# The first MLP unit of a convolution-attention kernel: the GELU of hidden block 0 moved behind the second group's outputs

## The chip, the cores and the metric

The kernel runs on one core of a Trainium2 chip. The metric is device time in microseconds (us) of one whole execution; the figure for a kernel is the median of its runs. All times inside an execution are counted from the start of the profiled span.

## The reference

The computation is two layers on an image batch `x` of 2 x 512 x 32 x 32 in float32. Layer 0 is an attention with deformed sampling points and a learned position bias, followed by an MLP over the channels. Layer 1 is a plain self-attention over the 1024 positions. The change lies in the MLP of layer 0:

```python
xn2 = _bn(x, bn2_g, bn2_b)
h1 = gelu(einsum('bchw,oc->bohw', xn2, mlp_w1) + mlp_b1, approximate=False)
return x + einsum('bchw,oc->bohw', h1, mlp_w2) + mlp_b2
```

`mlp_w1` is 2048 x 512 and `mlp_w2` is 512 x 2048, so the MLP takes 512 channels to 2048 hidden ones and back, for 2 images of 1024 positions.

## The kernel before

**Units.** The work goes attention of layer 0 (about 1900 us), its output projection, the MLP, then layer 1. The MLP is cut into eight units: image `b` (2) by hidden quarter `p` (4 quarters of 512 hidden channels). The loop at `for i, (b, p) in enumerate(units)` calls `layer1` for the 512 hidden channels and `layer2` for their share of the output. The change concerns unit 0 only, where `early` is true (`i == 0`).

**Products by quarters.** Every matrix product here is a 2 x 2 block product done with seven block products instead of eight, the operands being sums and differences of the quarters. Products are numbered 1 to 7, and `PARTS` says which two operands belong to each. A hidden quarter is kept in the tile `hm`, as `c11, c12, c21, c22` (256 channels by 512 positions each), with two more blocks, `r5` and `r3`, for partial results. `c11` is block 0, `c21` is block 2.

**Two levels in `layer1`.** Outer product 2 is done plainly: in unit 0 by `first`, which runs before everything else and copies its result into `r3` (L1133). The six other outer products go in three groups of two, (1,6), (4,7), (5,3), called groups 0, 1 and 2 below. For a group, `twice` runs seven inner products, called q1 to q7, on TensorE (L160), each 2 matmuls of 128x128 by 256 positions; a float32 matmul shows as two records in the profile, so a q is 4 records. The results lie in two PSUM tiles for each group, and the q's are added up in PSUM: q6 is added onto q1's result, q7 onto q6's, q4 onto q7's; q5 and q3 share the other tile with q2. So each result is read out before the next is added: q1 by ScalarE (L166), q2 by VectorE, q6 by ScalarE (L170), q7 by ScalarE (L172) and VectorE, q4 by ScalarE (L176), q3 by VectorE. For group 2 the target of these reads is `r5` and `r3`.

**What follows a group.** `done(0)` adds `c11` to `c12`. `done(1)` makes `c22`, then `c21`, and calls `gelu(2)`, `done(2)` makes the rest and calls `gelu(3)` and `gelu(1)`. A `gelu` is two ScalarE activations of 128x512 (L1092). In unit 0, `merge` adds `r3` (the result of outer product 2) to `c11` on VectorE, and calls `gelu(0)`.

**What sets the order.** Each step has a due time: the inner products have `7 * group + STEPS`, and further steps are put in by `fills`, a list of pairs of a due time and a function. All are sorted by due time and then written out:

```python
STEPS = ((0, 1), (1, 2), (3, 6), (4, 5), (6, 7), (9, 4), (12, 3))
todo = [(7 * g + t, g, q) for g in range(len(sets)) for t, q in STEPS]
todo += [(t, None, fill) for t, fill in fills]
for _, g, q in sorted(todo, key=lambda e: e[0]):
    with tc.issue_after(newest(mybir.EngineType.PE)):
```

So `merge` at 13.5 stands between q7 of group 1 (13) and q1 of group 2 (14); q4 of group 1 is at 16, q6 of group 2 at 17, q3 of group 1 with `done(1)` at 19, q7 of group 2 at 20. A scheduler then sets the final order on each engine; each engine works through its own in that order. PSUM tiles come in turn from four buffers, so a new tile waits for the last reader of the one four before. In unit 0 the scheduler also puts matmuls of `layer2` (L1073) between the last inner products of group 2.

In the program as built, ScalarE's order around the change is: q7 of group 1 (L172), q4 of group 1 (L176), the load of the activation table for GELU, `gelu(0)` (two instructions), q1 of group 2 (L166), q6 of group 2 (L170), q7 (L172), q4 (L176), `gelu(2)`, `gelu(3)`, `gelu(1)`.

**Weights.** For the next unit, SyncE's queue loads `mlp_w1` (L982) and copies parts of it into `w1e` (L992), and GpSimd's queue forms sums in place by DMAs that add (L975). The copies wait until the current unit's matmuls have read `w1e` for the last time.

Of the kernel before, what the change touches and what calls it, by code (L numbers as in the profile page):

```python
# [57 lines left out]
def conv_seq_kernel(ctx: ExitStack, tc: tile.TileContext, x, xt, kst, pst, cst, vec, wsm, outw, w1, w2, wl, wlt, brow, out):  # L58
# [15 lines left out]
    def col(name, i=0):  # L74
        return vs[:, VOFF[name] + i : VOFF[name] + i + 1]
# [45 lines left out]
    def spread(x, which=range(4)):  # L121
        for i in which:
            if i % 2 == 0:
                o, u = ((4, 0), (1, 3))[i // 2]
                nc.vector.tensor_tensor(x[o], x[u], x[1], ALU.subtract)  # L125
            else:
                o, u, v = ((5, 4, 3), (6, 5, 2))[i // 2]
                nc.vector.scalar_tensor_tensor(x[o], x[u], -1.0, x[v], ALU.mult, ALU.subtract)
# [7 lines left out]
    def plus(out, a, b_, op=ALU.add):  # L136
        nc.vector.tensor_tensor(out, a, b_, op)  # L137
# [46 lines left out]
    def inner_w(w, we, at=slice(1, 7), e=slice(0, 6)):  # L184
        return [w[:, at, k, P * n : P * n + P] for k, n in AT_W] + [we[:, e, j, :] for j in range(3)]

    def inner_x(x, xe, at=slice(1, 7), e=slice(0, 6)):
        return [x[:, at, k, 256 * n : 256 * n + 256] for k, n in AT_X] + [xe[:, e, j, :] for j in range(3)]
# [779 lines left out]
    with ExitStack() as top, tc.tile_pool(name="wp", bufs=1) as wp:  # L968
# [100 lines left out]
        def product(w, x):  # L1069
            def go(ps, a, b_):  # L1070
                for m in range(2):
                    for k in range(2):
                        nc.tensor.matmul(  # L1073
                            ps[:, m, :], w[:, a, k, m * P : (m + 1) * P], x[:, b_, k, :],
                            start=(k == 0), stop=(k == 1),
                        )
            return go
# [11 lines left out]
        def layer1(p, we, w, xb, xe, hm, others=(), early=False):  # L1089
            def gelu(blk, src, scale=1.0):  # L1090
                for m in range(2):
                    nc.scalar.activation(  # L1092
                        hm[:, blk, m, :], src[:, m, :], AF.Gelu,
                        bias=col("mb1", 4 * p + 2 * (blk // 2) + m), scale=scale,
                    )

            c11, c12, c21, c22, r5, r3 = (hm[:, j] for j in range(6))

            def weights(q, j):
                a = FIRST_W[PARTS[q][0]]  # L1100
                return [inner_w(w, we, a, a - 1)[j]]

            def moving(q, j):
                b_ = FIRST_X[PARTS[q][1]]
                return [inner_x(xb, xe, b_, b_ - 1)[j]]

            def dest(g, m, h):
                return hm[:, 2 * g : 2 * g + 2, m, 256 * h : 256 * h + 256]

            def done(g):  # L1110
                if g == 0:
                    plus(c12, c12, c11)
                elif g == 1:
                    plus(c22, c22, c12)
                    plus(c21, c21, c22)
                    gelu(2, c21, -1.0)
                else:
                    plus(c22, c22, r5)
                    gelu(3, c22, -1.0)
                    plus(c12, c12, r5)  # L1120
                    plus(c12, c12, r3)
                    gelu(1, c12)

            def second():
                ps = mq.tile([P, 2, 512], F32, tag="ps2", name="sw")
                product(w, xb)(ps, 0, 0)
                plus(c11, c11, ps)
                gelu(0, c11)

            def first():  # L1130
                ps = mq.tile([P, 2, 512], F32, tag="ps2", name="sw")
                product(w, xb)(ps, 0, 0)
                nc.scalar.copy(r3, ps)  # L1133

            def merge():
                plus(c11, c11, r3)
                gelu(0, c11)

            plain = ((-1, first), (13.5, merge)) if early else ((21, second),)
            twice(mq, ((1, 6), (4, 7), (5, 3)), weights, moving, dest, done, (*plain, *others))  # L1140
            spread([hm[:, j] for j in range(7)])

# [52 lines left out]
        for i, (b, p) in enumerate(units):  # L1195
# [9 lines left out]
            wa, we, wb = wts.pop((b, p))  # L1205
            hm = cp.tile([P, 7, 2, 512], F32, tag="big", name="hm")
            layer1(p, we, wa, xb, xe, hm, ((4, lambda: part(1)), (10, lambda: part(2))) if p == 0 else (), i == 0)
            if i == NU:
                with tc.issue_after(newest(mybir.EngineType.DVE)):
# [384 lines left out]
```

## Time and profile before

| | |
|---|---|
| median of 3 runs | 2625.18 us (2624.24 to 2625.37) |
| profiled execution, its own time | 2626.42 us |
| span in the profile (first to last instruction) | 2624.7 us |
| TensorE busy | 2597.7 us, 99% |
| VectorE busy | 2308.9 us, 88% |
| ScalarE busy | 1748.3 us, 67% |
| GpSimd busy | 977.8 us, 37% |
| mean granted TensorE clock | 0.998 |

Busy times are summed over the span; the granted clock is a share of full speed. TensorE's idle time is found in the view of the waits, its place in the timeline, and what it hung on in the chain of waits, which follows the last instruction back to what released it. In the timeline a row is: start, duration, engine, line, operation, output <- input, shape, count, and in brackets the idle time just before with what ended it. PEld is TensorE's loading of weights.

### The profile page before, as it was taken

What the parts mean: (1) busy time and instruction counts of PE and PEld (TensorE: products, weight loads), DVE (VectorE), ACT (ScalarE), POOL (GpSimd) and SP (SyncE); (2) the same over time, 40 slices, a digit from 0 to 9 for tenths busy, and PEclk for the clock granted to TensorE, in tenths of its full rate; (3) what the DMA queues carried; (4) which work ended last, traced back from release to release, by engine and by line L of the source; (5) the groups of instructions that cost most, each with busy time, mean ns of one, the idle gap of its engine ahead of it and who ended that gap; (6) DMA issues with size and microseconds to landing.
All of it is one profiled execution on the core that took longest, in us unless ns stands there. A gap on an engine that the chain in (4) does not pass through costs nothing.

```text
span 2624.7 us, 48900 instructions
## 1 busy us (share of the span) xinstructions
PE 2597.7 (99%) x19648; PEld 1005.3 (38%) x19648; DVE 2308.9 (88%) x1462; ACT 1748.3 (67%) x2325; POOL 977.8 (37%) x1121
## 2 busy tenths in 40 slices
PE   9999999999999999999999999999999999999999
PEld 3332322232333233322333332332355665646556
DVE  7999999999999999999999999898776587666656
ACT  5887898888887888888787777777633242224041
POOL 1344544444444444444444444333422333200100
PEclk9999999999999999999999999999999999999999
DMA  5898988999999999899898999787777768400202
GB/s 189 173 193 186 214 181 183 197 193 206 189 191 195 190 204 193 182 188 202 187 203 182 194 193 195 162 181 166 155 195 160 155 139 177 90 16 0 73 0 56
DMA packets 177522, 428.27 MB, mean 163 GB/s; under 512 B 29936, under 2 KB 78208, under 8 KB 174608
## 3 DMA queue, kind: packets, MB, share of 16 engines
q0 software_dynamic: 107392, 273.09, 58.1%
q1 hardware_dynamic: 69472, 151.75, 17.4%
q8 instruction: 155, 2.54, 0.4%
q14 instruction: 71, 0.58, 0.1%
q10 hardware_dynamic: 432, 0.31, 0.0%
HBM read 82.16 MB, written 6.55 MB: 34 GB/s over the span
## 4 chain that ended last, share of the span: by engine, by line
PE 75%; DVE 10%; issue 7%; DMA 4%; POOL 2%; ACT 2%; DVEq 0%; ACTq 0%; POOLq 0%; SPq 0%
PE ps L693 47%; PE sw L1073 7%; PE sw L160 7%; PE sw L1244 7%; DVE h L676 4%; PE sw L1020 2%; PE sw L1342 2%; DVE ub L713 2%; DMA u<-uc 1%; POOL u L732 1%; PE psg L595 1%; DMA u<-u 1%; PE sim L823 1%; DVE uo L713 1%; DVE hm L137 1%
## 5 line engine op out<-in xcount | busy, mean ns | idle before, releaser
L693 PE MATMUL ps<-h,cw 128*32 128x512 f32 x16384 | 1774.9, 593 | 10.8 <-ACT rx L703 7.9
L676 DVE CUSTOM_DVE_ANT_1 h<-ta,tb 128x4096 f32<-128x4096 f32 (+1 forms) x257 | 1131.0, 4402 | 20.3 <-PE ps L693 16.8
L693 PEld LDWEIGHTS ps<-h,cw 128*32 128x32 f32 x16384 | 525.9, 110 | 1228.8 <-issue 1134.5
L703 ACT ACTIVATE rx<-ps,sc 128x1024 f32<-128x1024 f32 x512 | 568.3, 1110 | 159.6 <-PE ps L693 100.1
L732 POOL DMA_DIRECT2D u<-u x397 | 409.1, 1511 | 15.0 <-DMA u<-ub 12.1
L705 ACT ACTIVATE ub<-ps,sc 128x1024 f32<-128x1024 f32 x256 | 308.2, 1204 | 83.8 <-PE ps L693 83.4
L713 DVE SCALAR_TENSOR_TENSOR ub<-rx,sc,ub 128x1024 f32<-128x1024 f32 x256 | 327.2, 1278 | 10.5 <-ACT ub L705 10.5
L715 POOL DMA_DIRECT2D uo<-ub x127 | 112.5, 886 | 582.8 <-DVE ub L713 536.0
L1073 PE MATMUL sw<-hm,w2t 128*128 128x512 f32 x448 | 194.3, 593 | 0.2 <-DVE hm L125 0.2
L705 ACT ACTIVATE uo<-ps,sc 128x1024 f32<-128x1024 f32 x128 | 154.1, 1204 | 42.1 <-PE ps L693 41.0
L713 DVE SCALAR_TENSOR_TENSOR uo<-rx,sc,uo 128x1024 f32<-128x1024 f32 x128 | 163.6, 1278 | 5.0 <-ACT uo L705 5.0
L732 POOL DMA_DIRECT2D u<-uc x126 | 126.3, 1246 | 23.5 <-DMA u<-uc 22.0
L715 POOL DMA_DIRECT2D uc<-ub x64 | 56.9, 889 | 196.9 <-DVE ub L713 156.0
L137 DVE TENSOR_TENSOR hm<-hm,sw 128x512 f32<-128x512 f32 x79 | 57.6, 732 | 79.0 <-PE sw L160 54.4
L1073 PEld LDWEIGHTS sw<-hm,w2t 128*128 128x128 f32 x448 | 84.9, 190 | 103.9 <-issue 97.3
L715 POOL DMA_DIRECT2D u<-ub x64 | 56.6, 884 | 167.5 <-DVE ub L713 163.9
L732 POOL DMA_DIRECT2D uc<-uo x63 | 100.3, 1593 | 21.1 <-DMA uc<-uo 20.8
L732 POOL DMA_DIRECT2D uc<-uc x63 | 106.3, 1688 | 2.3 <-DMA uc<-ub 2.3
L1408 POOL DMA_DIRECT2D xs<-rs x6 | 7.2, 1200 | 258.8 <-DVE rs L137 258.8
L656 ACT ACTIVATE ta<-fb,vs 128x512 f32<-128x512 f32 (+1 forms) x65 | 89.7, 1382 | 6.8 <-DMA fb<-fdr 6.8
L732 POOL DMA_DIRECT2D u<-uo x63 | 85.4, 1355 | 20.6 <-DMA u<-uo 16.2
L705 ACT ACTIVATE uc<-ps,sc 128x1024 f32<-128x1024 f32 x64 | 77.0, 1203 | 22.4 <-PE ps L693 14.1
(295 smaller groups left out, 2621.9 us busy)
## 6 DMA issues: line engine op xcount, KB each, us to landing
uo<-ub POOLq DMA_DIRECT2D x127, 512.0 KB, 5.4
fb<-fdr SPq DMA_DIRECT2D x64, 512.0 KB, 6.2
u<-ub POOLq DMA_DIRECT2D x64, 512.0 KB, 6.5
uc<-ub POOLq DMA_DIRECT2D x64, 512.0 KB, 6.1
u<-u POOLq DMA_DIRECT2D x63, 256.0 KB, 7.0
u<-uo SPq DMA_DIRECT2D x63, 256.0 KB, 5.7
u<-uo POOLq DMA_DIRECT2D x63, 256.0 KB, 7.1
uc<-uc POOLq DMA_DIRECT2D x63, 256.0 KB, 7.9
```

The source lines that it names most:

```text
L137: nc.vector.tensor_tensor(out, a, b_, op)
L160: nc.tensor.matmul(bank[:, e, :], w, x, start=(q in (1, 2, 5) and e == k == 0), stop=True, skip_group_check=True,)
L656: nc.scalar.activation(ta.rearrange("p j x -> p x j")[:, :, j0:j1], fb[:, 0, :, j0:j1], AF.Identity, bias=col("cb1"), scale=col("w1x"),)
L676: nc.vector._custom_dve(TENSOR_ADD_SAT, out=h1[:, y : y + step].rearrange("p y t x -> p (y t x)"), in0=a.unsqueeze(1).to_broadcast([P, ste ...
L693: nc.tensor.matmul(ps[32 * q : 32 * q + 32, h, :], cw2[:, 32 * z : 32 * z + 32], h1[:, 16 * h : 16 * h + 16, q, :], start=True, stop=True,)
L703: nc.scalar.activation(o, ps, AF.Relu, bias=sc[:, 4 + z : 5 + z])
L705: nc.scalar.activation(o, ps, AF.Relu, bias=sc[:, 4 + z : 5 + z], scale=sc[:, z : z + 1])
L713: nc.vector.scalar_tensor_tensor(r[1], r[0], sc[:, z : z + 1], r[1], ALU.mult, ALU.add)
L715: nc.gpsimd.dma_start(out=sums[s][1], in_=sums[s][3], accum_op=ALU.add)
L732: nc.gpsimd.dma_start(out=out, in_=in_, accum_op=ALU.add)
L1073: nc.tensor.matmul(ps[:, m, :], w[:, a, k, m * P : (m + 1) * P], x[:, b_, k, :], start=(k == 0), stop=(k == 1),)
L1244: nc.tensor.matmul(ps[:, m, :], w[:, a, k, c + m * P : c + (m + 1) * P], x[b_][:, k, :], start=(k == 0), stop=(k == nk - 1),)
```

## The change

In unit 0, `merge` is split: the addition of `r3` to `c11` keeps its due time of 13.5, and `gelu(0)` gets a due time of its own, 19.5, behind `done(1)` at 19 and ahead of q7 of group 2 at 20. Nothing is added or removed in the computation, and the other seven units are untouched.

```diff
-            def merge():
-                plus(c11, c11, r3)
-                gelu(0, c11)
-
-            plain = ((-1, first), (13.5, merge)) if early else ((21, second),)
+            plain = ((21, second),)
+            if early:
+                plain = (-1, first), (13.5, lambda: plus(c11, c11, r3)), (19.5, lambda: gelu(0, c11))
             twice(mq, ((1, 6), (4, 7), (5, 3)), weights, moving, dest, done, (*plain, *others))
             spread([hm[:, j] for j in range(7)])
```

In the program as built, the order changes on ScalarE alone, and there in one place: after q4 of group 1 come now q1 of group 2 (L166), the table load, the first half of `gelu(0)`, q6 of group 2 (L170), the second half of `gelu(0)`, and then q7 (L172) as before. `gelu(2)` still follows q4 of group 2. The instructions on TensorE, VectorE, GpSimd and SyncE keep their order. L166 now waits itself for the addition on VectorE, since it overwrites `r3`.

## Prediction

> **What bounds the kernel now.** I read the page's busy shares first, then TensorE's waits, then the chain of waits and the timeline around the change, and last the granted clock in a few stretches.
>
> ```profile
> span 2624.7 us, 48900 instructions
> PE 2597.7 (99%) x19648; PEld 1005.3 (38%) x19648; DVE 2308.9 (88%) x1462; ACT 1748.3 (67%) x2325; POOL 977.8 (37%) x1121
> ```
>
> TensorE is busy 99% of the span: only what takes idle time from it, or lets it run faster, shortens the kernel. Its waits (total us, times, longest):
>
> ```profile
> PE ps L693 <- ACT rx L703: 7.9, 14, 1.9
> PE sw L160 <- ACT hm L166: 3.8, 1, 3.8
> ```
>
> The longest single wait of the whole execution is 3.8 us, once, and it lies at the change. The chain of waits from 1955 to 1990 us shows what it hung on:
>
> ```profile
> 1954.98 7.35 PE sw L160 x34
> 1962.34 0.02 issue
> 1962.36 0.60 ACT hm L176
> 1962.96 0.02 issue
> 1962.97 1.28 ACT L1092
> 1964.26 0.01 issue
> 1964.27 1.33 ACT hm L1092 x2
> 1965.60 0.48 ACT hm L166
> 1966.08 0.04 issue
> 1966.12 6.39 PE sw L160 x16
> 1972.52 1.00 PE sw L1073 x2
> ```
>
> TensorE stops at 1962.32. ScalarE then does four things in a row: q4 of group 1 (L176), the table load, both halves of gelu(0), and q1 of group 2 (L166), on which q6 of group 2 is to be added. The reader is to see that TensorE waits only for the last of these. Also that 16 records then take 6.39 us, 0.40 each, where the 34 before take 7.35, 0.216 each. The stretches (length, busy time of each engine, granted clock, DMA) tell why:
>
> ```profile
> 1811.14:1814.55 3.41, 1.52 (x16) 0.29 (x12) 2.53 (x3) 1.98 (x2) 2.50 (x3) 1.00 1.08 201
> 1961.33:1964.74 3.41, 0.99 (x5) 0.54 (x3) 1.33 (x2) 2.35 (x3) 0.85 (x1) 1.00 0.41 71
> 1964.74:1968.15 3.41, 2.02 (x5) 1.67 (x6) 0.69 (x1) 1.33 (x3) 0.00 (x0) 0.50 0.31 52
> 1968.15:1971.57 3.42, 3.42 (x10) 2.70 (x9) 0.00 (x0) 0.59 (x1) 0.00 (x0) 0.50 0.00 0
> ```
>
> From 1964.74 to 1971.57 the clock is 0.50. The wait costs twice: once as idle time, once as a slow restart. The wait of 1.89 us in the first row (TensorE busy 1.52 of 3.41) left the clock at 1.00.
>
> **What the Trainium skill says.** "TensorE: Matmul & The Clock Gate", Part 1, says that TensorE's clock halves after a free-running window of about 3.4 us with little activity and returns after one busy window. The trace agrees: the slow stretch is 6.83 us, two windows, after a window busy for 0.99 us; a window busy for 2.02 us did not end it. "ScalarE: Activation LUTs", What ACT_TABLE_LOAD costs, gives 1283 ns for a table load, as here (1.28 us), and a drain of 1380 ns, of which nothing shows: GELU starts 0.01 us behind the load. "Perfetto Trace Analysis", Tensor Engine Instruction, says that ScalarE and VectorE work strictly in order, and TensorE pulls only weight loads ahead. So L166 could not pass gelu(0); the trace shows it standing there.
>
> **The change, part by part.** It adds and removes no instruction. Of the three moved (the table load and gelu(0)'s two activations), none issues a DMA; the built order of TensorE, VectorE, GpSimd and SyncE is unchanged.
>
> *L166 ahead of the load and gelu(0).* L176 ends at 1962.96. L166 must now wait itself for the addition of r3, which runs on VectorE from 1961.44 for 1.22, to 1962.66: it is done. L166 takes 0.59 (0.562 to 0.592 in the three seen nearby), 1962.97 to 1963.56; with the 0.04 seen before, TensorE resumes at 1963.60 instead of 1966.12: **2.52 us** less idle time. The wait falls to about 1.28 us, inside the 1.89 that kept the clock.
>
> *The slow restart.* At full clock the 16 records to the end of q7 of group 2 take 16 x 0.216 = 3.46, to 1967.06. The next matmul (L1073, layer2's product 1) takes the buffer that VectorE frees by reading q3 of group 1. Before, the timeline has it begin at 1972.39 (the chain's 1972.52 is the modelled end of the record ahead), 0.99 after q3's last record gave way to the next at 1971.40. Now q3 is through after 12 records, at 1963.60 + 2.59 = 1966.19; plus 0.99 is 1967.18. So this matmul moves from 1972.39 to 1967.18, by 5.21 us: the 2.52 above and **2.69 us** from the clock.
>
> *What is now late behind gelu(0)'s first half.* The load runs 1963.56 to 1964.84, the first half (0.71) to 1965.56. q6's evacuation L170 is queued behind it; it was ready about 1.1 us after q6 began (1.17 and 1.06 in groups 0 and 1), at 1964.7. It runs 1965.56 to 1966.15, and q7 of group 2, which waits for it, is due on TensorE at 1966.19: cost nothing, by 0.04 us. If that cover fails, the wait is at most the 0.85 us by which L170 starts late. The second half ends at 1966.87; its readers are layer2's product 1 with its second half, after 1967.18 + 0.86 + 0.86, and L172, ready at 1966.19 + 1.16 = 1967.35. Both are covered, by 2.0 and 0.5 us. VectorE's read of q2, which q5 waits for, runs 1963.59 to 1964.28, q5 is due at 1964.46.
>
> *Whether the gain lasts.* gelu(2) began 3.96 us after q3 of group 1 (1971.40 to 1975.36), nearly all VectorE work; it would end at 1966.19 + 3.96 + 1.33 = 1971.5, and its product was reached at about 1977.8, now 1972.6. The copies of unit 1's `w1e` start behind the last read of `w1e` (1975.94 before, SyncE at 1976.13), so they move along. The in-place sums of `w1t` have fixed times, the last issued at 1962.91, and land some 3.3 us later, at 1966.2; the copies now come at 1970.9. To the end of the MLP and beyond TensorE's waits behind 1980 sum to 1.6 us, all on VectorE, which moves along. So I give nothing back.
>
> The sum is -5.21 us against the profiled execution (2626.42 us in all, 2624.7 of it span, 1.72 around it). The median of the timed runs is 1.24 lower; the same difference gives 2625.18 - 5.21 = **2620.0 us**. The bound of 0.2%, about what a measurement of this kernel can tell from no change, is 5.25 us here: the forecast lies on it.
>
> **The unknown: the clock's window.** An execution may have its windows elsewhere. A boundary 0.39 to 1.7 us ahead of the restart gives two slow windows, and a loss of half of 6.83 less that, 2.6 to 3.2 us (the profile's was 1.38 ahead, 2.7); one slow window costs 3.41 / 2 = 1.7; with the wait shared evenly between two windows there may be no drop, 0. I take the profile's, and keep 0 and 3.2 as ends; a loss below nothing is excluded, as the new wait is shorter.
>
> **The rivals.** (1) *One slow window* in most timed runs: gain 2.5 + 1.7 = 4.2, 2621.0 us. For it: the median lies 1.24 below the profiled execution; against it: profiling itself may cost that. (2) *Only the idle time goes* (no drop in the timed runs, or the clock still falls at 1.28 us): 2622.7. Against it: the row at 1811. (3) *Slower: gelu(0) really runs behind gelu(2)*, as the due times are written. Then product 1, due at 1967.18, waits for gelu(2) to end at 1971.5 and gelu(0)'s 1.33, to 1972.9; q4 and q3 of group 2 stand behind it. That is 5.7 us of wait and, being above 3.8, a new slow restart of 2.7: 8.4 lost for 5.2 gained, 2628.4. It decides once gelu(0) is later than 1972.4. Against it: the built order has gelu(0) around L170, ahead of L172. (4) *Nothing moves*, because the freed time is lost to a later wait, such as w1e's landing: 2625.2. Against it: that chain follows TensorE.
>
> **How the numbers follow.** Two slow windows saved, 5.1 to 5.7: 0.57, of which 0.45 above the bound. One window: 0.28. Idle time only: 0.08. Slower: 0.04. Nothing: 0.03. So faster 0.45, same 0.51, slower 0.04. The range goes from 5.7 and some noise of the runs (0.5) to just short of the case of idle time only: 2618.9 to 2622.4.
>
> **What would show it.** In the profile after, TensorE's wait on L166 should be about 1.3 us; L166 should start at about 1962.97, the table load behind it; no stretch around 1966 with clock 0.50; L1073's first matmul at about 1967.2; the span near 2619.5. A new wait of TensorE on L170, or a longer one on gelu, would make it wrong, as would a half clock that stays.

## The result, and the profile after

| | before | after |
|---|---|---|
| median of 22 runs each, us | 2625.17 (2623.59 to 2626.99) | 2620.51 (2619.63 to 2622.44) |
| span of the profiled execution, us | 2624.7 | 2618.7 |

The ratio of after to before is 0.9983, with a 95% interval of 0.9976 to 0.9989: 4.66 us less, 0.18%. The interval, 2.9 to 6.3 us, excludes no change; it does not tell whether the gain is above or below 0.2%.

The page of after opens with the same shares, and with one instruction more than before. That one is a semaphore instruction of ScalarE at L166, which now waits itself for the addition on VectorE:

```profile
span 2618.7 us, 48901 instructions
PE 2596.1 (99%) x19648; PEld 1003.4 (38%) x19648; DVE 2310.0 (88%) x1462; ACT 1746.8 (67%) x2325; POOL 981.0 (37%) x1121
```

TensorE's waits (total us, times, longest). The wait on L166 is down from 3.8 to 1.2 us, and none on L170 has come in its place:

```profile
PE ps L693 <- ACT rx L703: 7.9, 14, 1.9
...
PE sw L160 <- ACT hm L166: 1.2, 1, 1.2
```

The chain of waits around the change (start, length, what):

```profile
1954.81 7.57 PE sw L160 x35
1962.38 0.02 issue
1962.40 0.35 ACT hm L176
1962.75 0.15 issue
1962.89 0.59 ACT hm L166
1963.48 0.04 issue
1963.53 3.72 PE sw L160 x16
1967.25 1.04 PE sw L1073 x2
```

The table load and gelu(0) have left the chain; only L176 and L166 stand in it. The 16 records take 3.72 us instead of 6.39. The clock stays at 1.00 (stretches: length, busy time of PE, PEld, DVE, ACT, POOL, granted clock, DMA):

```profile
1960.38:1963.79 3.41, 2.25 (x11) 1.67 (x10) 2.60 (x4) 1.40 (x4) 0.83 (x1) 1.00 0.68 117
1963.79:1967.20 3.41, 3.41 (x17) 2.73 (x16) 1.15 (x3) 2.80 (x4) 0.85 (x1) 1.00 0.45 77
```

ScalarE's timeline shows where the load and gelu(0) went (the bracket is idle time just before):

```profile
1962.40 0.60 ACT L176 ACTIVATE hm<-sw 128x512 f32<-128x512 f32 x1 [1.99 <-PE sw L160]
1962.89 0.58 ACT L166 COPY hm<-sw 128x512 f32<-128x512 f32 x1
1963.49 1.28 ACT L1092 ACT_TABLE_LOAD   x1
1964.79 0.72 ACT L1092 ACTIVATE hm<-hm,vs 128x512 f32<-128x512 f32 x1
1965.41 0.57 ACT L170 COPY hm<-sw 128x512 f32<-128x512 f32 x1
1965.88 0.72 ACT L1092 ACTIVATE hm<-hm,vs 128x512 f32<-128x512 f32 x1
```

They lie beside TensorE's 16 records, which run from 1963.53 on. L170 ends at about 1966.0, and q7 of group 2 (the third row here) starts at 1966.22 with no wait:

```profile
1963.53 1.99 PE L160 MATMUL sw<-xe,w1e 128*128 128x256 f32 x8 [1.16 <-ACT hm L166]
1965.36 1.03 PE L160 MATMUL sw<-xb,w1e 128*128 128x256 f32 x4
1966.22 1.03 PE L160 MATMUL sw<-xb,w1x 128*128 128x256 f32 x4
1967.16 1.12 PE L1073 MATMUL sw<-hm,w2t 128*128 128x512 f32 x2
```

**A measure for one place.** Whole executions scatter by 3 us, more than most effects here. So I compare one stretch: from the end of q4 of group 1 on TensorE (0.02 us before L176 starts; in before and after TensorE stops there) to the first matmul of unit 1, as the chain has them. It holds the same matmuls in every kernel without spare work. Its end, in the chains of before and of after:

```profile
1998.42 4.79 PE sw L160 x21
1993.19 9.97 PE sw L160 x45
```

Before it is 36.08 us (1962.34 to 1998.42), after it is 30.81 (1962.38 to 1993.19): 5.27 less. The two profiled spans differ by 6.0. The other 0.7 is not the change's: TensorE's waits on VectorE in L137 behind 1975 sum to 0.9 us in the first profile of before and to 0.2 in after, but in another execution of the kernel before (b2, below) they are 0.2 too.

### The profile page after: what moved, and what is told of

It is laid out like the page before. It is cut to its first block, busy times and chain, and to the rows that moved or that the text cites. A ratio compares the mean times of both kernels' runs of the same rounds, so it can differ in the third digit from the quotient of the medians.

```text
span 2618.7 us, 48901 instructions
## 1 busy us (share of the span) xinstructions
PE 2596.1 (99%) x19648; PEld 1003.4 (38%) x19648; DVE 2310.0 (88%) x1462; ACT 1746.8 (67%) x2325; POOL 981.0 (37%) x1121
## 4 chain that ended last, share of the span: by engine, by line
PE 67%; DVE 12%; issue 9%; DMA 6%; POOL 4%; ACT 2%; DVEq 0%; SPq 0%; POOLq 0%; ACTq 0%
PE ps L693 39%; PE sw L1073 7%; PE sw L160 7%; PE sw L1242 7%; DVE h L676 4%; DMA u<-uc 3%; DVE ub L713 2%; POOL u L732 2%; PE sw L1020 2%; PE sw L1340 2%; PE psg L595 1%; DVE uo L713 1%; DMA u<-uo 1%; PE sim L823 1%; DMA u<-u 1%
## 5 line engine op out<-in xcount | busy, mean ns | idle before, releaser
L1073 PE MATMUL sw<-hm,w2t 128*128 128x512 f32 x448 | 194.4, 593 | 0.3 <-DVE hm L125 0.2
L732 POOL DMA_DIRECT2D u<-uc x126 | 126.9, 1272 | 19.5 <-DMA u<-uc 18.3
L1073 PEld LDWEIGHTS sw<-hm,w2t 128*128 128x128 f32 x448 | 84.8, 190 | 104.4 <-issue 97.4
L137 DVE TENSOR_TENSOR hm<-hm,sw 128x512 f32<-128x512 f32 x79 | 57.6, 732 | 74.1 <-PE sw L160 51.7
```

Of the source, the lines that this page charges most:

```text
L732: nc.gpsimd.dma_start(out=out, in_=in_, accum_op=ALU.add)
L1073: nc.tensor.matmul(ps[:, m, :], w[:, a, k, m * P : (m + 1) * P], x[:, b_, k, :], start=(k == 0), stop=(k == 1),)
```

## The experiments

The theory: the wait of 3.8 us cost its idle time and a slow restart, and it came from L166 standing behind the table load and gelu(0). The rivals: the slow records have another cause, so only idle time counts; or gelu(0)'s own place is what matters. Line numbers shift in some kernels: L171 in e1 and L167 in e2 and e6 are L166; L181 in e1 is L176; L165 and L161 are L160; L1078 and L1074 are L1073. Times are compared with the kernel before as it ran beside each experiment. The edits are shown in their main lines.

### e1_fill: the same wait, filled with spare matmuls

```diff
+                for _ in range(spare if (g, q) == (2, 6) else 0):
+                    nc.tensor.matmul(
+                        held[1][:, 1, 0:256], weights(5, 0)[0], moving(5, 0)[0], start=True, stop=True,
+                        skip_group_check=True,
+                    )
```

The base is the kernel before; `spare` is a new argument of `twice`, 7 in unit 0 and 0 elsewhere.

> The kernel before, with its order of gelu(0) ahead of L166, and seven spare 128x256 matmuls into an unused half of a PSUM tile between q4 of group 1 and q6 of group 2; nobody reads them. They wait for L176 (1962.96) and last 14 records, to about 1966.0. Theory (idle time and clock): q6 still starts at about 1966.12, but at full clock, so layer2's first matmul moves from 1972.39 to about 1969.7, 2.7 us in the profile; the median falls by 1.7 to 2.7 (2622.5 to 2623.5), by what the timed runs lose to the clock. Rival (only the idle time counts, the 16 slow records are slow for another reason, such as VectorE or ScalarE): 2625.2, first L1073 at 1972.4.

Measured: 2623.92 us against 2625.47 for before in the same batch, ratio 0.9994 (0.9986 to 1.0003). That is 1.55 us less, a little short of the 1.7 to 2.7 expected, and by time alone it is unclear whether anything changed. The chain of waits settles it:

```profile
1961.80 0.61 ACT hm L181
1962.40 0.04 issue
1962.45 3.29 PE sw L159 x14
1965.74 3.55 PE sw L165 x16
1969.29 1.04 PE sw L1078 x2
```

ScalarE's timeline has the order of before:

```profile
1963.71 1.33 ACT L1097 ACTIVATE hm<-hm,vs 128x512 f32<-128x512 f32 x2
1964.95 0.56 ACT L171 COPY hm<-sw 128x512 f32<-128x512 f32 x1
```

L159 is the spare work, L1097 gelu(0). L166 still stands behind gelu(0), and q6 starts no earlier than before relative to the stop. But the 16 records now take 3.55 us instead of 6.39, at clock 1.00, and the stretch is 33.45 us, 2.63 less than 36.08. Nothing but TensorE's activity was changed, so the slow restart is the clock's, and costs about what the forecast gave it for this profile (2.69).

### e2_table: the table load taken out of the wait

```diff
             def first():
+                with tc.issue_after(newest(mybir.EngineType.Activation)):
+                    nc.scalar.activation(tg, xb[:, FIRST_X[3], 1, 0:1], AF.Gelu)
                 ps = mq.tile([P, 2, 512], F32, tag="ps2", name="sw")
```

The base is the kernel before; `tg` is a new tile of one element in each partition.

> The kernel before, with a one-element GELU ahead of `first`, so that the table load falls into ScalarE's idle time before 1949; its result is not read. gelu(0) and L166 keep their order, and the wait shrinks by the load's 1.28 us to 2.5, between the 1.89 that kept the clock and the 3.80 that did not. Theory: 1.28 us of idle time, and 2.7 more only if the clock holds: 2621.2 if it holds, 2623.9 if it falls. Rival (only idle time): 2623.9 with no slow stretch to be seen, or with the slow stretch and still no effect.

Measured: 2623.14 us, ratio 0.9990 (0.9984 to 0.9997), between the two times expected. The wait is 2.38 us. TensorE's timeline, then the stretches of this profile:

```profile
1964.16 3.07 PE L161 MATMUL sw<-xe,w1e 128*128 128x256 f32 x8 [2.38 <-ACT hm L167]
```

```profile
1961.51:1964.92 3.41, 1.03 (x6) 0.69 (x5) 1.29 (x2) 2.29 (x4) 0.85 (x1) 1.00 0.39 67
1964.92:1968.34 3.42, 3.42 (x10) 2.67 (x9) 0.00 (x0) 0.58 (x1) 0.00 (x0) 0.50 0.40 69
```

The wait fell whole into one window, TensorE was busy for 1.03 us of it, and the next window ran at half clock: one window, not two. The stretch is 33.72. Taking the load away alone, with L166 still behind gelu(0), leaves 2.9 us more than the change does.

This is one execution. Each timed execution has its mean granted clock on record, to three places, and 7 of the 21 of this kernel have 1.000. A slow window of 3.41 us would take the mean over 2622 us below 0.9994, which reads 0.999, so in these 7 the clock held. The same order of instructions thus lowers the clock in some executions and not in others.

### e4_late: gelu(0) really behind gelu(2)

```diff
+            def late():
+                with tc.issue_after(newest(mybir.EngineType.Activation)):
+                    gelu(0, c11)
-                plain = (-1, first), (13.5, lambda: plus(c11, c11, r3)), (19.5, lambda: gelu(0, c11))
+                plain = (-1, first), (13.5, lambda: plus(c11, c11, r3)), (19.5, late)
```

The base is the kernel after.

> The kernel after, with gelu(0) held behind gelu(2) by a dependency, as the due times are written. In the built order ScalarE then does L166, L170, L172, L176 of group 2, the table load, gelu(2), gelu(0), and TensorE no longer has product 1 of layer2 to put between q7, q4 and q3 of group 2. Forecast's rival 3 (product 1 waits where it stood, for gelu(0) to end at 1972.9, and the clock falls again): 2628.4. Worked from the built order: q4 waits 0.9 us for L172, product 2 waits 1.4 us for gelu(2), each too short for the clock: some 2.2 us slower than after, about 2622.7.

Measured: 2624.12 us, ratio 0.9995 (0.9987 to 1.0003) to before; against after, each taken from the before of its own batch, 3.3 us slower, where 2.2 was expected from the built order and 2628.4 us from rival 3. The stretch is 33.71, 2.90 above after's. TensorE's timeline:

```profile
1963.37 1.99 PE L160 MATMUL sw<-xe,w1e 128*128 128x256 f32 x8 [1.16 <-ACT hm L166]
1965.20 1.03 PE L160 MATMUL sw<-xb,w1e 128*128 128x256 f32 x4
1966.07 1.03 PE L160 MATMUL sw<-xb,w1x 128*128 128x256 f32 x4
1967.78 1.13 PE L160 MATMUL sw<-xe,w1x 128*128 128x256 f32 x4 [0.69 <-ACT hm L172]
1968.87 1.13 PE L160 MATMUL sw<-xb,w1e 128*128 128x256 f32 x4
1971.63 0.70 PE L1073 MATMUL sw<-hm,w2t 128*128 128x512 f32 x1 [1.64 <-ACT hm L1092]
```

There are two new waits, 0.69 for L172 (expected 0.9) and 1.64 for gelu(2) (expected 1.4), where after had product 1 of layer2 to do. The table load makes part of the second: in this order it stands behind L176 of group 2 (ScalarE runs it from 1969.56 to 1970.84). The clock held through all three waits. So gelu(0) can come too late as well, but the price is 3 us, not the forecast's 8.4.

### e6_spare_table and e3_spare: the rest of the wait

```diff
-                nc.scalar.copy(r3, ps)
+                nc.scalar.copy(hm[:, 6], ps)
-                plain = (-1, first), (13.5, lambda: plus(c11, c11, r3)), (19.5, lambda: gelu(0, c11))
+                plain = (-1, first), (13.5, lambda: plus(c11, c11, hm[:, 6])), (19.5, lambda: gelu(0, c11))
```

The base is the kernel after; this edit is e3_spare, and e6_spare_table has the early table load of e2_table as well.

> The kernel after, with the result of outer product 2 kept in hm's seventh block instead of r3, so that L166 need not wait for the addition on VectorE and comes ahead of L176 in the built order; and the table load moved early as in the run above. Theory: what is left of the wait, 1.16 us in the profile after, goes, less about 0.2 for q5 behind VectorE's read of q2: about 1.0 us faster than after, 2619.5. Rival (after's remaining wait is covered by VectorE's chain, which sets the pace): 2620.5.

> As e6_spare_table, with the table load where it stands in after (behind L176, ahead of gelu(0)'s first half). L170 is queued behind the load and the first half, and q7 of group 2 now comes 1.2 us earlier than in after: the cover that the forecast gave L170 (0.04 us) is gone. Theory: a wait of TensorE on L170 of 0.3 to 0.6 us appears, and the site is that much longer than in e6_spare_table; the median, 2620.5, can't tell it. Rival (L170 is not what q7 waits for): no such wait, equal to e6_spare_table.

Measured: e6_spare_table 2620.15 us (expected 2619.5), ratio to its before 0.9980 (0.9971 to 0.9988); e3_spare 2620.04 (2620.5), 0.9981 (0.9973 to 0.9989). In both, L166 runs ahead of L176, and TensorE's wait on it is gone. The stretch is 29.77 in e6_spare_table, 1.04 less than after, and 30.19 in e3_spare. The two differ by the place of the table load, and by that of one layer2 matmul in TensorE's built order. In e3_spare TensorE waits 0.21 us for L170 (0.3 to 0.6 was expected), which is queued behind the load and gelu(0)'s first half; that wait, and the restart behind it, lie in the 0.42 us between the two. The chain of e3_spare:

```profile
1961.74 1.28 ACT L1092
1963.03 0.01 issue
1963.04 0.72 ACT hm L1092
1963.76 0.48 ACT hm L170
1964.24 0.04 issue
1964.29 1.13 PE sw L160 x4
```

So the load is hidden in after, where TensorE restarts later, and no longer quite hidden here. Both are faster than after in this stretch, by 1.0 and 0.6 us; in time neither can be told from it.

### e5_before_spare: gelu(0) left where it was

The same block for the result of `first`, in the kernel before: `copy(hm[:, 6], ps)`, and in `merge` `plus(c11, c11, hm[:, 6])`. The due times stay as they were.

> The kernel before, due times untouched (gelu(0) at 13.5), only with the result of outer product 2 kept in hm's seventh block. The built order then puts L166 ahead of L176 by itself, and both halves of gelu(0) ahead of L170. Theory (what counts is that L166 does not stand behind gelu(0)): the wait on L166 and the slow stretch are gone; a wait of some 0.9 us on L170 or on VectorE's read of q3 stays, too short for the clock: about 2621.0. Rival (gelu(0) itself must come later, as in the change): 2625.2.

Measured: 2620.93 us, ratio 0.9983 (0.9975 to 0.9990), the change's own ratio. The stretch is 30.75, against 30.81 in after. ScalarE's timeline, and the one wait of TensorE in this place:

```profile
1960.45 0.59 ACT L166 COPY hm<-sw 128x512 f32<-128x512 f32 x1 [0.26 <-PE sw L160]
1962.18 0.60 ACT L176 ACTIVATE hm<-sw 128x512 f32<-128x512 f32 x1 [1.14 <-PE sw L160]
1962.80 1.28 ACT L1092 ACT_TABLE_LOAD   x1
1964.09 1.33 ACT L1092 ACTIVATE hm<-hm,vs 128x512 f32<-128x512 f32 x2
1965.33 0.56 ACT L170 COPY hm<-sw 128x512 f32<-128x512 f32 x1
```

```profile
PE sw L1073 <- ACT hm L170: 0.8, 1, 0.8
```

Both halves of gelu(0) still run in one piece, ahead of L170. The wait on L166 is gone altogether, as in e3_spare; in its place stands the wait of 0.83 us on L170, of a matmul of layer2 that the scheduler here puts ahead of q7 of group 2. That the two kernels come out alike is therefore a coincidence of two sums, but the loss of before is gone in both. What mattered was L166's place. The rival of idle time alone fell with e1_fill; this run removes the one of gelu(0)'s own place.

### b1 to b5: where the clock's windows fall

Five more profiled executions of the kernel before, unchanged.

> The kernel before once more, to see where the clock's windows fall. Theory: windows 3.41 us long that start anywhere, so the wait of 3.8 us costs half of 3.41 or half of up to 6.83 beside its idle time: the stretch from TensorE's stop to the first matmul of unit 1 is 36.1 us with two slow windows and about 35.1 with one. Rival (the loss is the same each time): 36.1.

> As b1: 36.1 us from TensorE's stop to unit 1 with two slow windows, about 35.1 with one; the rival, 36.1 each time.

> The kernel before once more, to count how often its wait costs one slow window of the clock and how often two. The forecast gave two windows twice the chance of one (0.57 to 0.28); a stretch of 36.1 us from TensorE's stop to unit 1 is two, 35.1 is one, 33.4 none.

> As b3: 36.1 us is two slow windows, 35.1 one, 33.4 none. If the share of the timed runs is the forecast's, two of three looks show two; if the median gain of 4.66 us is a mixture led by one window, most show one.

> As b3 and b4: 36.1 us two slow windows, 35.1 one, 33.4 none.

Measured: the wait is 3.80 us in all. The table has the first profile too; "fall" is the time from TensorE's stop to the moment when the clock goes to 0.50, in all six as the trace has it.

| | whole time, us | 16 records, us | stretch, us | fall, us | slow windows |
|---|---|---|---|---|---|
| first | 2626.42 | 6.39 | 36.08 | 2.40 | 2 |
| b1 | 2626.66 | 5.41 | 35.14 | 4.58 | 1 |
| b2 | 2624.09 | 5.41 | 35.14 | 4.48 | 1 |
| b3 | 2625.24 | 6.38 | 36.08 | 2.37 | 2 |
| b4 | 2624.12 | 5.41 | 35.14 | 4.64 | 1 |
| b5 | 2623.74 | 5.41 | 35.13 | 4.58 | 1 |

So the rival, the same loss each time, is out. In b1 the windows lie so:

```profile
1960.65:1964.06 3.41, 2.22 (x11) 1.61 (x9) 2.56 (x3) 1.40 (x3) 0.68 (x2) 1.00 0.55 94
1964.06:1967.47 3.41, 0.80 (x4) 0.72 (x5) 0.69 (x1) 2.55 (x4) 0.63 (x1) 1.00 0.45 77
1967.47:1970.89 3.42, 3.42 (x10) 2.70 (x9) 0.00 (x0) 0.58 (x1) 0.00 (x0) 0.50 0.00 0
```

TensorE restarts at 1966.67, at full speed for 0.8 us; then one full window at half clock, and that window, all busy, ends it. One window costs 3.41 / 2 = 1.7 us, two cost 2.7. The same code is thus worth 4.33 us (35.14 - 30.81) or 5.27. Weighted by these six executions, four to two, that is 4.64; the medians say 4.66. So close a match is luck: six draws are few, and the interval of the gain holds either case alone. Nor do the six look like windows that start anywhere, as the theory has it: the fall comes at 2.4 us or at 4.5 to 4.6, and nowhere between. The cause of that is open.

The timed executions give more draws. Those of the six profiles with two slow windows have a mean clock of 0.998, those with one 0.999. Of 79 timed executions of the kernel before, in the two batches of the experiments, 18 have 0.998, 60 have 0.999 and one has 1.000. The rounding may hide some with two windows among the 0.999. But those with 0.998 took 0.9 us longer in one batch (median 2626.01 against 2625.08) and 1.3 in the other (2626.36 against 2625.10) where the stretches differ by 0.94. That fits one window in most of the others. With these shares, 5.27 us for two windows, 4.33 for one and the 2.64 of the shorter wait alone for none, the gain is an estimated 4.5 us.

## Why the prediction was right, and where it was off

The forecast was 2620.0 us, the measured median is 2620.51, and the parts came as follows.

**The path.** L166 ahead of the load, 1962.97 in the forecast, came at 1962.89, since it starts 0.11 us before L176 ends. TensorE resumed at 1963.53 (forecast 1963.60), and layer2's first matmul came at 1967.16 (1967.18). From the first profile's 1972.39 that is 5.23 us, with a stop only 0.04 later; the forecast said 5.21. That it fits to 0.02 is partly luck. TensorE resumed 0.07 earlier than forecast, the 12 records to the end of q3 took 2.69 us and not 2.59, and the matmul behind them came 0.94 later and not 0.99; the three cancel. "It adds and removes no instruction" missed the semaphore instruction at L166, which cost nothing that shows.

**The covers.** Each held: L170 in time for q7 with 0.2 us to spare (0.04 in the forecast), gelu(0)'s second half ended at 1966.60, before its readers, VectorE's read of q2 ended at 1964.20. e3_spare shows that L170's cover was real: with TensorE 1.2 us earlier, the wait is there. The 5.27 us in the stretch up to unit 1 says that nothing was given back there.

**The clock.** That the restart was slow because of the clock, and that a wait of 1.2 us would not bring it down, was argued from two rows of before; e1_fill and the profile after show it. One reading does not hold as it stands: the prediction finds the trace in agreement with "TensorE: Matmul & The Clock Gate", Part 1. That page has the clock halve after an idle window; here windows lowered it in which TensorE was busy for 0.69 (b2) to 1.03 (e2_table) of 3.41 us, so it need not be idle.

**The step that was off** is "The unknown: the clock's window" and the chances made from it. The forecast took the profile's two windows as the likeliest (0.57, against 0.28 for one). Of six profiled executions two show two windows and four show one, the timed ones lean the same way, and the median gain of 4.66 us lies between the two cases, about as near to rival (1), 4.2, as to the forecast. The sum of 5.21 was right for the execution it was made from; carried to the median it was 0.55 us too large. The clock's term, 2.7 there and mostly 1.7 elsewhere, is large enough to make that difference, though the interval of the medians is too wide to show that it did. The 1.24 us by which the median lay below the profiled execution, which the forecast weighed for rival (1), is a weak sign: b1, with one slow window, took longer still, 2626.66 us.

**Rival (3)** was priced wrongly. It took TensorE's order for granted, with q4 and q3 stuck behind product 1. In e4_late, where gelu(0) is held back, the scheduler orders TensorE anew too, and no wait there lowered the clock: 1.3 us below before in the medians (with no change inside its interval), not 3.2 above.

## What to carry to other kernels

Where an engine works in order, look at what stands ahead of the one short instruction that the bounding engine waits for; a table load and two activations that nobody needed yet made a wait of 1.2 us into 3.8. A wait of TensorE that lowers its clock is paid twice, so shortening it until the clock holds gains more than the idle time; read the granted clock behind each long wait. When the loss depends on where the clock's window falls, one profile gives one draw: profile several executions, and read the granted clock of the timed ones, before the sum is carried to the median.

## What the runs showed of the hardware that was not expected

- A wait of 2.38 us lowered the clock in the profile of e2_table, though not in all its timed executions; one of 1.89 us in before had not. In e2_table a window with 1.03 us of activity out of 3.41 did it, and the windows that did it in before and b1 had 0.99 and 0.80. The window of before with 1.52 did not; it is placed by counting 44 windows back from 1964.74, as no fall of the clock marks it.
- The fall need not come during the wait. In before it came 2.40 us into it, in b1 when TensorE had been running again for 0.8 us at full speed. Both fit a fall at the end of a window of 3.41 us, the length of the slow stretch in b1 and half of that in before.
- Three waits close together, 1.16, 0.69 and 1.64 us in e4_late, left the clock at 1.00. It is not shown that any two of them fell into one window.
